# Norm squares, zero masks and a bias of a graph and attention network's heads moved from VectorE to ScalarE and GpSimd

## The chip, the cores and the metric

The kernel runs on one core of a Trainium2 chip. The metric is the device time in microseconds of one execution; lower is better. The engines are named as the profile names them: PE (TensorE, matmuls), DVE (VectorE), ACT (ScalarE), POOL (GpSimd) and SP (SyncE, which here issues most DMAs).

## The reference

A two-layer network on 3327 nodes with 256 features. Layer 0 is a normalised graph convolution and a mixture of eight experts; layer 1 is a graph attention and the attention block that concerns us here. That block, cut to what matters, with 4 heads of width 64, 4 query experts a head, and the length s = 3327:

```
sx = einsum('bsh,ndh->bnsd', x, hl_w) + hl_b          # x is layer-normed first
pad = sx == 0
q, k, v = projections of sx
scores = einsum('bnesd,bntd->bnest', q, k) * d ** 0.5 + causal
qkv = einsum('bnest,bntd->bnesd', softmax(scores), v)
qkv = where(pad[:, :, None], 0.0, qkv)
gs = softmax(einsum('bnsf,nef->bnse', out, gate_w) + gate_b)
mixed = einsum('bnsed,bnse->bnsd', out, gs)
fx = layernorm(mixed + resid, ln_g, ln_b)              # over 64, for each head
pm = fx == 0
hx = relu(where(pm, 0.0, fx @ fc1_w.T + fc1_b))
hx = where(pm, 0.0, hx @ fc2_w.T + fc2_b)
hx = layernorm(hx + fx, fnorm_g, fnorm_b)
fg = softmax(fout @ fgate_w.T)
result = hx * fg, added to x
```

`layernorm` here is (x - mean) / sqrt(mean of squared deviations + 1e-8) over the 64 features of a head.

## The kernel before

The 3327 rows are padded to 26 tiles of 128 rows. The first third of the program does layer 0 and the graph attention of layer 1. The rest, the function `heads`, is what the change touches, and it follows them without overlap but for its constants.

In `heads` a unit is a row tile `t` and a head `h`; tiles go from 0 to 25, and because the attention is causal, tile `t` sees `t + 1` key tiles, which are cut into `t // 4 + 1` chunks of at most 512 keys. One pass of the main loop handles one chunk `k` and issues for it, in this order:

- `drain`: DVE copies the four score banks `pqk` (one for each query expert) from PSUM to the tile `sc` and takes the row maximum in the same instruction. It runs one unit ahead, since the maximum over all chunks of a unit (`anmax`) is needed before the exponentials.
- `attend`: PE multiplies the weights of chunk `k` with the values `vr` into `po`.
- `turn`: DVE transposes the weights of chunk `k + 1` in 32x32 blocks.
- `values` and `weigh`: SP loads `vr` for chunk `k + 2`; ACT computes its exponentials in place, two experts now and two later in the pass.
- if a unit ended in the pass before, `back`: PE turns the unit's output back (`ptO`), and ACT copies it out as `qkv` and `glp`.
- if a unit ends in this pass, `over`: ACT copies `po` to `ot`, and POOL multiplies `ot` by the zero mask `sxd`.
- one step of each open tail and preparation, in passes after which no unit's `back` is due, and in every pass for tiles below 8.
- the second half of `weigh`, and `fill`: PE computes the scores of a later chunk into `pqk`.

A preparation (`prepare`, for the next tile) loads the tile's rows, norms them (`xn`), transposes, projects to `sxt`, and makes keys `kt`, values `v`, queries `qt` and the mask `sxd`. The mask begins as a copy of `sxt` that four DMAs of SP spread over partitions; a DVE comparison with zero then turns it into ones and zeros. A tail (`tail`, for a tile whose four heads are done) is a generator of small steps: gate softmax (`gs`), mix to `fx`, norm `l1`, fully connected layer 1 (`h1`) and 2 (`p2`, `fo`), norm `l2`, final gate (`fg`), store. The last tile has its own `last_tail`, in two halves. As many as five tails are open at once: `back` steps them on while more than four are left, and then opens another.

All engines issue in program order: the class `InOrder` ties each instruction of an engine to the one before it, so an instruction that waits holds up all that follow on its engine. PSUM tiles of `heads` other than `po` rotate through four banks of one tag, which the scores and the small matmuls of tails and preparations share. The function `empty` copies from PSUM either by ACT or by DVE, whichever has the smaller running sum in `load`; the sums are the author's estimates in microseconds, added where instructions are issued:

```
if load["act"] + 0.14 + 0.00086 * n <= load["dve"] + 0.1 + 0.00112 * n:
```

The two norms of a tail (`norm4`) use DVE's statistics instructions, two for each of four heads, and then POOL for the power -0.5, the subtraction, and the three multiplications and additions. The zero masks of the fully connected layers are DVE instructions that compare with zero and multiply at once.

Of the kernel before, what the change touches and what calls it, by code (L numbers as in the profile page):

```python
# [12 lines left out]
F32 = mybir.dt.float32  # L13
# [4 lines left out]
AF = mybir.ActivationFunctionType  # L18
ALU = mybir.AluOpType
AX = mybir.AxisListType  # L20
PSUM = bass.MemoryType.PSUM

P = 128
# [3 lines left out]
D = 256  # L27
# [74 lines left out]
class Net:  # L102
# [766 lines left out]
    def heads(self, xs, vs, out):  # L869
        tc, a = self.tc, self.a  # L870
        nc = InOrder(tc)
        Q = 32
        with ExitStack() as ctx:
            one = ctx.enter_context(tc.tile_pool(name="at", bufs=1))
# [3 lines left out]
            tl = ctx.enter_context(tc.tile_pool(name="att", bufs=2))  # L878
            sm = ctx.enter_context(tc.tile_pool(name="atsm", bufs=4))
# [10 lines left out]
            load = dict(act=0.0, dve=0.0)  # L890

            def empty(dst, src, n, scale=None):
                if load["act"] + 0.14 + 0.00086 * n <= load["dve"] + 0.1 + 0.00112 * n:
                    load["act"] += 0.14 + 0.00086 * n
                    if scale is None:
                        nc.scalar.copy(dst, src)
                    else:
                        nc.scalar.mul(dst, src, scale)
                else:
                    load["dve"] += 0.1 + 0.00112 * n  # L900
                    if scale is None:
                        nc.vector.tensor_copy(dst, src)
                    else:
                        nc.vector.tensor_scalar(dst, src, scale, None, ALU.mult)

            def turned(src, dst):

                pt = ps.tile([P, 2, P], F32, tag="b", name="pt")
                for k in range(2):
                    nc.tensor.transpose(pt[:, k, :], src[:, ts(k, P)], self.ident)  # L910
                empty(dst, pt, D)

            def prepare(t, res):
# [7 lines left out]
                nc.vector.bn_stats(st, x)  # L924
                nc.vector.bn_aggr(mv, st)
                nc.vector.tensor_scalar(rs, mv[:, 1:2], 1e-5, None, ALU.add)
                nc.gpsimd.tensor_tensor(rs, rs, self.nhalf[:, :1], ALU.pow)
                load["dve"] += 0.7
                yield
                xn = self.work.tile([P, D], F32, tag="xn", name="xn2", bufs=1)  # L930
                nc.vector.tensor_scalar(xn, x, mv[:, 0:1], rs, ALU.subtract, ALU.mult)
                load["dve"] += 0.35
                yield
                xt = self.work.tile([P, 2, P], F32, tag="xt", name="xt2", bufs=1)
                turned(xn, xt)
# [8 lines left out]
                for c in range(2):  # L944
                    nc.scalar.activation(
                        sxt[:, c, :], pp[:, c, :], AF.Identity, bias=hlb[:, c : c + 1]
                    )
                load["act"] += 0.6
                yield

                sxd = self.work.tile([P, 4, P], F32, tag="sxd", name="sxd", bufs=3)
                for k in range(2):
                    for s in range(2):
                        nc.sync.dma_start(
                            out=sxd[ds(64 * k, 64), s::2, :], in_=sxt[ds(64 * s, 64), :, :]
                        )
                pp = ps.tile([P, 4, 64], F32, tag="b", name="pv")
                for c in range(2):
# [32 lines left out]
                for s in range(2):  # L991
                    empty(qt[:, s::2, :, :], pp[s], BLK, 8.0)
                yield
                nc.vector.tensor_scalar(sxd, sxd, 0.0, None, ALU.not_equal)
                load["dve"] += 0.4
                sx = tl.tile([P, D], F32, tag="sx", name="sx", bufs=5)
                turned(sxt.rearrange("p c q -> p (c q)"), sx.rearrange("p (c q) -> p c q", c=2))
                res.update(sx=sx, sxd=sxd, qt=qt)
# [80 lines left out]
            def turn(u, g):  # L1079
# [4 lines left out]
                nc.vector.transpose(w, w)  # L1084
                load["dve"] += 0.1 + 0.00417 * n


            po = ps_o.tile([P, 4, BLK], F32, tag="po", name="po")
            po = po[:, :, :P].rearrange("p q (e i) -> p q e i", e=4)
# [54 lines left out]
            def rows(v):  # L1144

                return v.unsqueeze(1).to_broadcast([P, 4, 64])

            def softmax4(g, n, tag):

                g3 = g.rearrange("p (n e) -> p n e", e=4)  # L1150
                m = sm.tile([P, n], F32, tag=tag + "m", name=tag + "m")
                s = sm.tile([P, 4 * n], F32, tag=tag + "s", name=tag + "s")
                s3 = s.rearrange("p (n e) -> p n e", e=4)
                nc.vector.tensor_reduce(m, g3, AX.X, ALU.max)
                nc.vector.tensor_tensor(s3, g3, m.unsqueeze(2).to_broadcast([P, n, 4]), ALU.subtract)
                yield
                nc.scalar.activation(s, s, AF.Exp)
                yield
                nc.vector.tensor_reduce(m, s3, AX.X, ALU.add)
                nc.vector.reciprocal(m, m)  # L1160
                nc.vector.tensor_tensor(s3, s3, m.unsqueeze(2).to_broadcast([P, n, 4]), ALU.mult)
                load["dve"] += 0.6
                load["act"] += 0.25
                return s

            def norm4(v, g, b, tag):

                mv = sm.tile([P, 4, 2], F32, tag=tag + "mv", name=tag + "mv")
                for h in range(4):
                    st = sm.tile([P, 6], F32, tag=tag + "st", name=tag + "st")  # L1170
                    nc.vector.bn_stats(st, v[:, ts(h, 64)])
                    nc.vector.bn_aggr(mv[:, h, :], st)
                rs = sm.tile([P, 4], F32, tag=tag + "rs", name=tag + "rs")
                nc.vector.tensor_scalar(
                    rs, mv.rearrange("p h s -> p s h")[:, 1, :], 1e-8, None, ALU.add
                )
                load["dve"] += 1.1
                nc.gpsimd.tensor_tensor(rs, rs, self.nhalf[:, :4], ALU.pow)
                v3 = v.rearrange("p (h d) -> p h d", h=4)
                nc.gpsimd.tensor_tensor(v3, v3, mv[:, :, 0:1].to_broadcast([P, 4, 64]), ALU.subtract)  # L1180
                nc.gpsimd.tensor_tensor(v3, v3, rs.unsqueeze(2).to_broadcast([P, 4, 64]), ALU.mult)
                nc.gpsimd.tensor_tensor(v3, v3, rows(g), ALU.mult)
                nc.gpsimd.tensor_tensor(v3, v3, rows(b), ALU.add)

            def tail(t, sx, qkv, glp, den):
# [13 lines left out]
                nc.vector.tensor_tensor(gl, gl, gb, ALU.add)  # L1199
                load["dve"] += 0.9  # L1200
                gs = yield from softmax4(gl, 4, "gs")
                nc.vector.tensor_tensor(gs, gs, rd, ALU.mult)
                mx = qkv.rearrange("p h e d -> p (h e) d")
                nc.gpsimd.tensor_tensor(
                    mx, mx, gs.unsqueeze(2).to_broadcast([P, 16, 64]), ALU.mult
# [7 lines left out]
                nc.gpsimd.tensor_tensor(fx, fx, sx, ALU.add)  # L1213
                yield
                yield
                norm4(fx, lng, lnb, "l1")
                yield
                yield
                fxt = tl.tile([P, 2, P], F32, tag="fxt", name="fxt", bufs=2)
                turned(fx, fxt)  # L1220
                yield
                h1 = tl.tile([P, 2, P], F32, tag="h1", name="h1")
                ph = ps.tile([P, 2, P], F32, tag="b", name="ph1")
                for c in range(2):
                    nc.tensor.matmul(ph[:, c, :], fc1, fxt[:, c, :], start=True, stop=True)
                nc.scalar.activation(h1, ph, AF.Relu, bias=fb1)
                load["act"] += 0.4
                yield
                nc.vector.scalar_tensor_tensor(h1, fxt, 0.0, h1, ALU.not_equal, ALU.mult)
                load["dve"] += 0.4  # L1230
                yield
                p2 = ps.tile([P, D], F32, tag="b", name="ph2")
                for c in range(2):
                    nc.tensor.matmul(p2[:, ts(c, P)], h1[:, c, :], fc2, start=True, stop=True)
                fo = tl.tile([P, D], F32, tag="fo", name="fo", bufs=3)
                nc.vector.tensor_tensor(
                    fo.rearrange("p (h d) -> p h d", h=4),
                    p2.rearrange("p (h d) -> p h d", h=4), rows(fb2), ALU.add,
                )
                nc.vector.scalar_tensor_tensor(fo, fx, 0.0, fo, ALU.not_equal, ALU.mult)  # L1240
                load["dve"] += 0.8
                nc.gpsimd.tensor_tensor(fo, fo, fx, ALU.add)
                yield
                yield
                norm4(fo, fng, fnb, "l2")
                yield
                yield
                fot = tl.tile([P, 2, P], F32, tag="fxt", name="fot", bufs=2)
                turned(fo, fot)
                x = tl.tile([P, D], F32, tag="xend", name="xend", bufs=2)  # L1250
                nc.sync.dma_start(out=x, in_=xs[ts(t, P), :])
                yield
                pg = ps.tile([P, 4], F32, tag="b", name="pfg")
# [8 lines left out]
            def last_tail(t, c, sx, r):  # L1262
# [4 lines left out]
                if c == 0:  # L1267
                    r["fx"] = tl.tile([P, D], F32, tag="fx", name="fx", bufs=3)
                    r["fo"] = tl.tile([P, D], F32, tag="fo", name="fo", bufs=3)
                    r["fot"] = tl.tile([P, 2, P], F32, tag="fotl", name="fotl", bufs=1)  # L1270
                    x = r["x"] = tl.tile([P, D], F32, tag="xend", name="xend", bufs=2)
                    nc.sync.dma_start(out=x, in_=xs[ts(t, P), :])
                fx, fo, fot = r["fx"][:, half], r["fo"][:, half], r["fot"][:, c, :]

# [39 lines left out]
                    AX.X, ALU.add,  # L1314
                )
                nc.vector.tensor_tensor(gl, gl, gb[:, ds(8 * c, 8)], ALU.add)
                gs = yield from softmax4(gl, 2, "lgs")
                nc.vector.tensor_tensor(gs, gs, rd, ALU.mult)
                yield
                mx = qkv.rearrange("p h e d -> p (h e) d")  # L1320
# [11 lines left out]
                yield  # L1332
                ph = ps.tile([P, P], F32, tag="b", name="ph1")
                nc.tensor.matmul(ph, fc1, fxt, start=True, stop=True)
                h1 = tl.tile([P, P], F32, tag="h1", name="h1")
                nc.scalar.activation(h1, ph, AF.Relu, bias=fb1)
                yield
                nc.vector.scalar_tensor_tensor(h1, fxt, 0.0, h1, ALU.not_equal, ALU.mult)
# [15 lines left out]
                pg = ps.tile([P, 4], F32, tag="b", name="pfg")  # L1354
                for k in range(2):
                    nc.tensor.matmul(pg, fot[:, k, :], fgw[:, k, :], start=(k == 0), stop=(k == 1))
                fg = yield from softmax4(pg, 1, "fg")
                f3 = fo.rearrange("p (h d) -> p h d", h=4)
                nc.vector.tensor_tensor(f3, f3, fg.unsqueeze(2).to_broadcast([P, 4, 64]), ALU.mult)
                nc.vector.tensor_tensor(fo, fo, x, ALU.add)  # L1360
# [629 lines left out]
```

## Time and profile before

| | us |
|---|---|
| median of 3 runs (3046.64 to 3051.62) | 3050.26 |
| the profiled execution, its own time | 3033.66 |
| its span, first to last instruction | 3032.0 |
| busy in the span: PE / DVE | 2702.8 / 2506.5 |
| busy in the span: ACT / POOL | 1678.2 / 886.5 |

The mean granted TensorE clock of the profiled execution is 0.973. `heads` begins at about 972 us of the span, where the first rows are loaded as `xres`, so it fills about two thirds of it. All instructions of the ordered engines carry line 61 of the program, that of the `InOrder` helper, so groups are told apart by the names of their tiles: `sc<-pqk` is a drain, `sc<-sc` on DVE a transpose and on ACT an exponential, `po<-sc,vr` an attend. A line of a group gives the number of instructions, their busy time, the mean duration in ns, and the idle time of the engine just before them with what ended it. A line of waits gives the total in us, how many there were, and the longest.

### The profile page before, as it was taken

To read this page: it belongs to the slowest core of one execution; us is meant where nothing else is said; L and a number is where in the kernel's file an instruction comes from. 1 tells how busy PE (TensorE), PEld (TensorE's weight loads), DVE (VectorE), ACT (ScalarE), POOL (GpSimd) and SP (SyncE) were. 2 spreads that over 40 slices of the span, in tenths; PEclk is the share of its full clock that TensorE was granted. 3 is DMA by queue.
4 is the path that set the end of the run, shared out by engine and by line. 5 is a ranking of instruction groups with operands and counts; after the bars stand their busy time and mean duration, and the time that the engine had idled before them with its cause. 6 is when DMAs were issued, how large, how long until landed. Compare 5 with 4: busy or idle time off the path is not lost.

```text
span 3032.0 us, 126726 instructions
## 1 busy us (share of the span) xinstructions
PE 2702.8 (89%) x54254; PEld 2004.2 (66%) x54254; DVE 2506.5 (83%) x6203; ACT 1678.2 (55%) x4570; POOL 886.5 (29%) x1178
## 2 busy tenths in 40 slices
PE   7999988788899789998999998899989999999885
PEld 6878877667677666666666666666656666666554
DVE  5103643789997689999999999999999999999996
ACT  6410144555554556565666665666656666566664
POOL 6441644711322254432332221222121111111121
PEclk9999999889999889999999999999999999999998
DMA  9994578567773223333333343333333433433332
GB/s 376 356 314 134 190 240 261 199 212 253 247 266 99 67 74 110 95 95 104 111 99 106 104 120 105 99 111 105 111 107 104 116 107 114 116 111 106 113 106 74
DMA packets 258194, 449.81 MB, mean 148 GB/s; under 512 B 58816, under 2 KB 156608, under 8 KB 257504
## 3 DMA queue, kind: packets, MB, share of 16 engines
q1 hardware_dynamic: 245536, 417.50, 44.6%
q0 software_dynamic: 6576, 18.02, 1.6%
q8 instruction: 428, 7.01, 1.0%
q10 hardware_dynamic: 5520, 6.18, 0.6%
q14 instruction: 134, 1.10, 0.1%
HBM read 393.37 MB, written 25.88 MB: 138 GB/s over the span
## 4 chain that ended last, share of the span: by engine, by line
DVE 48%; PE 19%; issue 2%; ACT 1%; DMA 0%; POOL 0%; SPq 0%; DVEq 0%; POOLq 0%; ACTq 0%
DVE sc L61 40%; PE po L61 7%; PE pqk L61 6%; PE acc L61 2%; PE ptO L61 1%; DVE fo L61 1%; DVE l2mv L61 1%; DVE l1mv L61 1%; ACT sc L61 0%; PE pq L61 0%; DVE anmax L61 0%; DVE gl L61 0%; DVE l2st L61 0%; PE psxt L61 0%; DVE l1st L61 0%
## 5 line engine op out<-in xcount | busy, mean ns | idle before, releaser
L61 ACT ACTIVATE sc<-sc,anmax 128x512 f32<-128x512 f32 (+3 forms) x1568 | 1041.1, 670 | 124.1 <-DVE anmax L61 123.9
L61 DVE TENSOR_SCALAR_CACHE_REDUCE sc<-pqk 128x512 f32<-128x512 f32 (+3 forms) x1568 | 897.9, 626 | 52.8 <-PE pqk L61 50.9
L61 PEld LDWEIGHTS po<-sc,vr 32*64 32x64 f32 x43728 | 666.0, 131 | 337.7 <-DVE sc L61 195.5
L61 PE MATMUL po<-sc,vr 32*64 32x128 f32 x43728 | 769.2, 276 | 117.2 <-DVE sc L61 74.2
L61 PE MATMUL pqk<-kt,qt 64*128 64x512 f32 (+3 forms) x3136 | 800.4, 581 | 44.6 <-DVE sc L61 17.1
L61 DVE STREAM_TRANSPOSE sc<-sc 128x2048 f32<-128x2048 f32 (+3 forms) x392 | 816.1, 2082 | 12.9 <-ACT sc L61 12.9
L61 PEld LDWEIGHTS pqk<-kt,qt 64*128 64x128 f32 x3136 | 314.4, 187 | 232.4 <-issue 80.0
L61 PE MATMUL acc<-wh,p 128*128 128x259 f32 x1352 | 310.0, 387 | 34.6 <-DVE p L61 34.5
L61 PEld LDWEIGHTS acc<-wh,p 128*128 128x128 f32 x1352 | 254.2, 191 | 92.7 <-DVE p L61 51.9
L61 PE MATMUL acc<-y,pan 128*128 128x256 f32 x1352 | 301.3, 382 | 11.9 <-DMA pan<-in_adjt_dram 10.2
L61 POOL TENSOR_TENSOR ot<-ot,sxd 128x512 f32<-128x512 f32 x103 | 131.7, 1279 | 611.1 <-ACT ot L61 600.8
L61 ACT ACTIVATION_READ_ACCUMULATOR sc<-sc,anmax 128x1 f32 x1568 | 302.1, 193 | 0.0
L61 PEld LDWEIGHTS acc<-y,pan 128*128 128x128 f32 x1352 | 256.0, 191 | 52.2 <-issue 17.5
L61 ACT ACTIVATE u<-u,d 128x512 f32<-128x512 f32 (+1 forms) x182 | 125.1, 688 | 159.5 <-DVE u L61 159.3
L61 ACT COPY qkv<-ptO 128x256 f32<-128x256 f32 x104 | 38.7, 373 | 222.9 <-PE ptO L61 222.9
L61 DVE SCALAR_TENSOR_TENSOR u<-bc,d 128x512 f32<-128x512 f32 (+1 forms) x182 | 135.8, 747 | 0.1
L61 DVE SCALAR_TENSOR_TENSOR p<-pan,u 128x512 f32<-128x512 f32 (+1 forms) x182 | 126.4, 694 | 10.0 <-PE acc L61 5.7
L61 PE MATMUL ptO<-igw,ot 128*128 128x68 f32 x832 | 116.4, 284 | 15.6 <-DVE sc L61 11.6
L61 DVE DVE_READ_ACCUMULATOR sc<-pqk 128x1 f32 x1568 | 128.6, 82 | 0.0
L61 PEld LDWEIGHTS ptO<-igw,ot 128*128 128x128 f32 x832 | 102.3, 193 | 34.8 <-issue 20.9
L61 ACT ACTIVATE junk<-ar 128x1664 bf16<-128x1664 f32 x52 | 82.7, 1591 | 66.7 <-DMA ar<-in_adj_dram 65.4
L61 PEld LDWEIGHTS <-own 64*128 64x128 bf16 x832 | 53.7, 95 | 94.5 <-issue 82.9
(324 smaller groups left out, 2872.5 us busy)
## 6 DMA issues: line engine op xcount, KB each, us to landing
vr<-vs SPq DMA_DIRECT2D x976, 128.0 KB, 2.6
ar<-in_adj_dram SPq DMA_DIRECT2D x104, 832.0 KB, 7.8
vr<-vs SPq DMA_DIRECT2D x544, 96.0 KB, 2.2
pan<-in_adjt_dram SPq DMA_DIRECT2D x156, 256.0 KB, 4.7
pan<-in_adjt_dram SPq DMA_DIRECT2D x26, 1024.0 KB, 10.7
pan<-in_adjt_dram SPq DMA_DIRECT2D x20, 832.0 KB, 4.7
w1e<-w SPq DMA_DIRECT2D x59, 256.0 KB, 2.5
took<-places SPq DMA_DIRECT2D x59, 129.0 KB, 5.0
```

Source lines behind the costliest of these rows:

```text
L61: made = make(*args, **kw)
```

## The change

The statistics of the two tail norms are replaced by one DVE sum for each norm (negated), four ACT Squares with accumulation (on 64 x - sum, so without a division first), and two scalings on POOL; the norm becomes a generator with two more steps. Every comparison with zero is made by ACT, as Square of Sign: for the mask `sxd` before the DMAs that spread it (a tile `nz` takes the place of `sxt` as their source), and for `fx` and `fxt` in a tile `nzf`, which POOL then multiplies in. POOL also takes the norming of `xn` (two instructions in place of one), the addition of the bias `fb2`, and three small multiplications of the softmaxes; `p2` is emptied by `empty`. The last tile's tail keeps its own way, with the softmax product on DVE. The tiles `h1` and `xend` have one buffer instead of two, and the last tile's `xend` is loaded by the second half of its tail instead of the first. The estimates added to `load` are changed to match.

```diff
+            def nonzero(dst, src):
+                nc.scalar.activation(dst, src, AF.Sign)
+                nc.scalar.activation(dst, dst, AF.Square)
+                load["act"] += 0.75
...
@@ prepare
                 nc.vector.tensor_scalar(rs, mv[:, 1:2], 1e-5, None, ALU.add)
+                load["dve"] += 0.7
+                yield
                 nc.gpsimd.tensor_tensor(rs, rs, self.nhalf[:, :1], ALU.pow)
-                load["dve"] += 0.7
-                yield
                 xn = self.work.tile([P, D], F32, tag="xn", name="xn2", bufs=1)
-                nc.vector.tensor_scalar(xn, x, mv[:, 0:1], rs, ALU.subtract, ALU.mult)
-                load["dve"] += 0.35
+                nc.gpsimd.tensor_tensor(xn, x, mv[:, 0:1].to_broadcast([P, D]), ALU.subtract)
+                nc.gpsimd.tensor_tensor(xn, xn, rs.to_broadcast([P, D]), ALU.mult)
...
+                nz = self.work.tile([P, 2, P], F32, tag="xn", name="nz", bufs=1)
+                nonzero(nz, sxt)
...
-                            out=sxd[ds(64 * k, 64), s::2, :], in_=sxt[ds(64 * s, 64), :, :]
+                            out=sxd[ds(64 * k, 64), s::2, :], in_=nz[ds(64 * s, 64), :, :]
...
-                nc.vector.tensor_scalar(sxd, sxd, 0.0, None, ALU.not_equal)
-                load["dve"] += 0.4
@@ softmax4 (last=False)
-                nc.vector.tensor_tensor(s3, s3, m.unsqueeze(2).to_broadcast([P, n, 4]), ALU.mult)
-                load["dve"] += 0.6
+                (nc.vector if last else nc.gpsimd).tensor_tensor(
+                    s3, s3, m.unsqueeze(2).to_broadcast([P, n, 4]), ALU.mult
+                )
+                load["dve"] += 0.4
@@ norm4
-                mv = sm.tile([P, 4, 2], F32, tag=tag + "mv", name=tag + "mv")
+                v3 = v.rearrange("p (h d) -> p h d", h=4)
+                ns = sm.tile([P, 4], F32, tag=tag + "ns", name=tag + "ns")
+                nc.vector.tensor_reduce(ns, v3, AX.X, ALU.add, negate=True)
+                load["dve"] += 0.35
+                yield
+                rs = sm.tile([P, 4], F32, tag=tag + "rs", name=tag + "rs")
                 for h in range(4):
-                    st = sm.tile([P, 6], F32, tag=tag + "st", name=tag + "st")
-                    nc.vector.bn_stats(st, v[:, ts(h, 64)])
-                    nc.vector.bn_aggr(mv[:, h, :], st)
-                rs = sm.tile([P, 4], F32, tag=tag + "rs", name=tag + "rs")
-                nc.vector.tensor_scalar(
-                    rs, mv.rearrange("p h s -> p s h")[:, 1, :], 1e-8, None, ALU.add
-                )
-                load["dve"] += 1.1
+                    nc.scalar.activation(
+                        sq, v[:, ts(h, 64)], AF.Square, bias=ns[:, h : h + 1], scale=64.0,
+                        accum_out=rs[:, h : h + 1],
+                    )
+                load["act"] += 1.2
+                yield
+                nc.gpsimd.tensor_scalar(ns, ns, 1 / 64, None, ALU.mult)
+                nc.gpsimd.tensor_scalar(rs, rs, 1 / 64**3, 1e-8, ALU.mult, ALU.add)
                 nc.gpsimd.tensor_tensor(rs, rs, self.nhalf[:, :4], ALU.pow)
-                nc.gpsimd.tensor_tensor(v3, v3, mv[:, :, 0:1].to_broadcast([P, 4, 64]), ALU.subtract)
+                nc.gpsimd.tensor_tensor(v3, v3, ns.unsqueeze(2).to_broadcast([P, 4, 64]), ALU.add)
@@ tail
-                nc.vector.tensor_tensor(gs, gs, rd, ALU.mult)
+                nc.gpsimd.tensor_tensor(gs, gs, rd, ALU.mult)
...
-                norm4(fx, lng, lnb, "l1")
+                yield from norm4(fx, lng, lnb, "l1")
...
                 turned(fx, fxt)
-                yield
-                h1 = tl.tile([P, 2, P], F32, tag="h1", name="h1")
+                nz = tl.tile([P, 2, D], F32, tag="nzf", name="nzf", bufs=1)
+                nonzero(nz[:, 0, :], fx)
+                yield
+                nonzero(nz[:, 1, :], fxt.rearrange("p c q -> p (c q)"))
+                h1 = tl.tile([P, 2, P], F32, tag="h1", name="h1", bufs=1)
...
-                nc.vector.scalar_tensor_tensor(h1, fxt, 0.0, h1, ALU.not_equal, ALU.mult)
-                load["dve"] += 0.4
+                nc.gpsimd.tensor_tensor(
+                    h1, h1, nz[:, 1, :].rearrange("p (c q) -> p c q", c=2), ALU.mult
+                )
...
-                nc.vector.tensor_tensor(
-                    fo.rearrange("p (h d) -> p h d", h=4),
-                    p2.rearrange("p (h d) -> p h d", h=4), rows(fb2), ALU.add,
-                )
-                nc.vector.scalar_tensor_tensor(fo, fx, 0.0, fo, ALU.not_equal, ALU.mult)
-                load["dve"] += 0.8
+                empty(fo, p2, D)
+                f3 = fo.rearrange("p (h d) -> p h d", h=4)
+                nc.gpsimd.tensor_tensor(f3, f3, rows(fb2), ALU.add)
+                nc.gpsimd.tensor_tensor(fo, fo, nz[:, 0, :], ALU.mult)
                 nc.gpsimd.tensor_tensor(fo, fo, fx, ALU.add)
...
-                norm4(fo, fng, fnb, "l2")
+                yield from norm4(fo, fng, fnb, "l2")
...
-                x = tl.tile([P, D], F32, tag="xend", name="xend", bufs=2)
+                x = tl.tile([P, D], F32, tag="xend", name="xend", bufs=1)
```

More of the change, by code (lines that the diff above doesn't have):

```diff
@@ L926, in prepare @@
                 nc.vector.tensor_scalar(rs, mv[:, 1:2], 1e-5, None, ALU.add)
-                nc.gpsimd.tensor_tensor(rs, rs, self.nhalf[:, :1], ALU.pow)
                 load["dve"] += 0.7
                 yield
+                nc.gpsimd.tensor_tensor(rs, rs, self.nhalf[:, :1], ALU.pow)
                 xn = self.work.tile([P, D], F32, tag="xn", name="xn2", bufs=1)
-                nc.vector.tensor_scalar(xn, x, mv[:, 0:1], rs, ALU.subtract, ALU.mult)
-                load["dve"] += 0.35
+                nc.gpsimd.tensor_tensor(xn, x, mv[:, 0:1].to_broadcast([P, D]), ALU.subtract)
+                nc.gpsimd.tensor_tensor(xn, xn, rs.to_broadcast([P, D]), ALU.mult)
                 yield
@@ L1085, in turn @@
                 load["dve"] += 0.1 + 0.00417 * n
+            sq = one.tile([P, 64], F32, name="sq")
             po = ps_o.tile([P, 4, BLK], F32, tag="po", name="po")
@@ L1146, in rows, with softmax4 @@
                 return v.unsqueeze(1).to_broadcast([P, 4, 64])
-            def softmax4(g, n, tag):
+            def softmax4(g, n, tag, last=False):
                 g3 = g.rearrange("p (n e) -> p n e", e=4)
@@ L1166, in norm4 @@
             def norm4(v, g, b, tag):
-                mv = sm.tile([P, 4, 2], F32, tag=tag + "mv", name=tag + "mv")
-                for h in range(4):
-                    st = sm.tile([P, 6], F32, tag=tag + "st", name=tag + "st")
-                    nc.vector.bn_stats(st, v[:, ts(h, 64)])
-                    nc.vector.bn_aggr(mv[:, h, :], st)
-                rs = sm.tile([P, 4], F32, tag=tag + "rs", name=tag + "rs")
-                nc.vector.tensor_scalar(
-                    rs, mv.rearrange("p h s -> p s h")[:, 1, :], 1e-8, None, ALU.add
-                )
-                load["dve"] += 1.1
+                v3 = v.rearrange("p (h d) -> p h d", h=4)
[4 more added lines that the diff above has]
+                rs = sm.tile([P, 4], F32, tag=tag + "rs", name=tag + "rs")
+                for h in range(4):
+                    nc.scalar.activation(
[6 more added lines that the diff above has]
+                nc.gpsimd.tensor_scalar(rs, rs, 1 / 64**3, 1e-8, ALU.mult, ALU.add)
                 nc.gpsimd.tensor_tensor(rs, rs, self.nhalf[:, :4], ALU.pow)
-                v3 = v.rearrange("p (h d) -> p h d", h=4)
-                nc.gpsimd.tensor_tensor(v3, v3, mv[:, :, 0:1].to_broadcast([P, 4, 64]), ALU.subtract)
+                nc.gpsimd.tensor_tensor(v3, v3, ns.unsqueeze(2).to_broadcast([P, 4, 64]), ALU.add)
                 nc.gpsimd.tensor_tensor(v3, v3, rs.unsqueeze(2).to_broadcast([P, 4, 64]), ALU.mult)
@@ L1270, in last_tail @@
                     r["fot"] = tl.tile([P, 2, P], F32, tag="fotl", name="fotl", bufs=1)
-                    x = r["x"] = tl.tile([P, D], F32, tag="xend", name="xend", bufs=2)
+                else:
+                    x = r["x"] = tl.tile([P, D], F32, tag="xend", name="xend", bufs=1)
                     nc.sync.dma_start(out=x, in_=xs[ts(t, P), :])
@@ L1316, in last_tail @@
                 nc.vector.tensor_tensor(gl, gl, gb[:, ds(8 * c, 8)], ALU.add)
-                gs = yield from softmax4(gl, 2, "lgs")
+                gs = yield from softmax4(gl, 2, "lgs", True)
                 nc.vector.tensor_tensor(gs, gs, rd, ALU.mult)
@@ L1334, in last_tail @@
                 nc.tensor.matmul(ph, fc1, fxt, start=True, stop=True)
-                h1 = tl.tile([P, P], F32, tag="h1", name="h1")
+                h1 = tl.tile([P, P], F32, tag="h1", name="h1", bufs=1)
                 nc.scalar.activation(h1, ph, AF.Relu, bias=fb1)
@@ L1356, in last_tail @@
                     nc.tensor.matmul(pg, fot[:, k, :], fgw[:, k, :], start=(k == 0), stop=(k == 1))
-                fg = yield from softmax4(pg, 1, "fg")
+                fg = yield from softmax4(pg, 1, "fg", True)
                 f3 = fo.rearrange("p (h d) -> p h d", h=4)
```

## The prediction

> **What bounds the kernel now.** I read the page's busy shares and slices, then busy time by stage, then the groups and waits of the longest stage, and last a timeline of single instructions.
>
> ```profile
> PE 2702.8 (89%) x54254; PEld 2004.2 (66%) x54254; DVE 2506.5 (83%) x6203; ACT 1678.2 (55%) x4570; POOL 886.5 (29%) x1178
> ...
> DVE  5103643789997689999999999999999999999996
> ...
> POOL 6441644711322254432332221222121111111121
> ```
>
> The mean shares name PE. The slices say otherwise for the last two thirds, which are the heads: there DVE is at 9 and POOL at 1 or 2. Busy time of each engine by stretch (columns PE, PEld, DVE, ACT, POOL):
>
> ```profile
> 960.00:1104.00 144.00, 118.46 (x1816) 92.82 (x1814) 94.02 (x305) 71.79 (x237) 45.52 (x47) 0.86 0.25 68
> 1104.00:1292.00 188.00, 171.59 (x3908) 123.77 (x3907) 172.63 (x515) 115.70 (x368) 95.21 (x110) 0.95 0.33 95
> 1292.00:2879.00 1587.00, 1448.55 (x40788) 987.98 (x40790) 1528.96 (x3676) 997.83 (x2975) 344.15 (x383) 0.99 0.37 108
> 2879.00:3032.00 153.00, 111.00 (x3536) 77.22 (x3534) 127.30 (x302) 81.12 (x241) 26.41 (x33) 0.92 0.31 90
> ```
>
> The third row is tiles 8 to 24, 17 of 26: DVE 96%, PE 91%, ACT 63%, POOL 22%. So DVE bounds it, with PE close behind. Rows 1 and 2 (tiles 0 to 7) have PE level with or above DVE; work taken from DVE there frees little. The waits of DVE, and then of PE, in the third stretch:
>
> ```profile
> DVE sc L61 <- PE pqk L61: 37.1, 51, 3.5
> ...
> PE po L61 <- DVE sc L61: 64.3, 88, 1.5
> PE po L61 <- issue: 19.6, 28, 1.4
> ```
>
> PE waits for DVE more than DVE for PE. Of the 1587 us, DVE has 1529 of work, 37 of waits for PE and 21 of gaps of tens of ns. PE has 1449 + 20 of its own issue gaps. One 512-wide chunk takes DVE 4.67 us (four drains of 0.61 start to start, a transpose of 2.23) and PE 4.08 (attend 2.09, fill 1.99), both read from the timeline at 2218 to 2228 us. What a tail or preparation adds to DVE comes after the transpose and delays the next drain. That is seen at the first norm of a tail:
>
> ```profile
> 2212.39 0.18 DVE L61 BATCH_NORM_STATS2 l1st<-fx 128x6 f32<-128x64 f32 x1
> 2212.61 0.18 DVE L61 BATCH_NORM_AGGREGATE l1mv<-l1st 128x2 f32<-128x6 f32 x1
> ...
> 2213.80 0.17 DVE L61 TENSOR_SCALAR l1rs<-l1mv 128x4 f32<-128x4 f32 x1
> 2213.88 0.68 DVE L61 TENSOR_SCALAR_CACHE_REDUCE sc<-pqk 128x512 f32<-128x512 f32 x1
> ```
>
> Nine small instructions push the drain back by 1.49 us.
>
> **What the Trainium skill says.** "GPSIMD Engine Reference", section Specifications: GpSimd shares its SBUF interfaces with VectorE and contends with VectorE instructions in a two-port mode or with two SBUF inputs. The trace agrees: at 1034.17 us the `gss` multiply on DVE took 1.16 us beside a POOL `ot` multiply of 1034.03 to 1035.31; alone it takes 0.17. Drains from PSUM and transposes keep their 0.61 and 2.23 beside POOL work. "ScalarE: Activation LUTs", section What ACT_TABLE_LOAD costs: an activation is 186 ns + 0.833 ns an element, 93 more for each pointer operand, 93 less back to back. By this a 512-wide Exp is 0.71; the trace has 715 ns. The same page, Table sets: simple functions lie in every set. The trace has five table loads of 1283 ns, none in the heads, and the instruction order of the changed kernel has the same five, so I charge Sign and Square no loads.
>
> **The change part by part**, for one tile in the third stretch.
>
> *Taken from DVE.* Durations are from DVE's groups there, less about 0.08 where an instruction starts inside its predecessor, plus 0.04 for its gap. Norm l1: 1.49. Norm l2: 1.65, as its `rs` averages 0.354 instead of 0.188. `xn` 0.45, `sxd` compare 0.41, `fo` add 0.39, `fo` mask 0.52, `h1` mask 0.40, `fgs` 0.22, `gss` multiplies 0.25 and 0.21. Sum 5.99 us.
>
> *Given to DVE.* Two reduces of 128x256 to 4. No such row exists: the 64-element reduce takes 0.27, the 256-wide statistics 0.40. I take 0.37 each, 0.74. Net 5.25; over 17 tiles 89 us. The balancer also moves 14 evacuations from ACT to DVE by the new order, mostly in tiles 0 to 7: 11 at 0.42 and 3 at 0.69, 6.7 us.
>
> *Given to ACT.* Six 256-wide Sign or Square, by that page's price an estimate of 0.31 to 0.40 each (2.0; a 256-wide copy shows 0.37), eight 64-wide Squares with accumulator at about 0.35 start to start (2.8; the 128-wide Exp with its read goes every 0.40), `fo` evacuation 0.3: 5.1 us a tile, 87 in the stretch. ACT goes from 63% to about 72%. Queued behind them are the second pair of Exps of each iteration, and behind those DVE's transpose; DVE waits 0.7 us in all for Exps now, and an iteration's Exps are 2.84 us of 4.67. If that cover fails, the price is the second rival's.
>
> *Given to POOL.* Two for `xn` (0.62 each by `fx<-fx,l1mv`), three 256-wide (0.73 each), seven tiny ones (0.2 to 0.4 by its one-element rows): 5.4 us a tile, 92 in the stretch, 22% to 29%. Hidden there; the POOL results are wanted one or two iterations later. In tiles 4 to 7 POOL goes from 51% to about 63%, and `ot`, for which the next iteration's `ptO` waits, queues behind tail work.
>
> *New waits.* Each norm has two more steps, so a tail takes 21 steps instead of 17; with at most five open no burst of forced steps arises. ACT's Squares wait for DVE's reduce, issued a step earlier: covered by an iteration. The preparation's `xn` now follows POOL's power and whatever POOL has queued: 0.9 us longer in tile 0, where nothing covers it, 0 to 5 us in tiles 1 to 4. SP issues the same transfers; the four for `sxd` wait 0.7 us longer for ACT, and the single `xend` buffer makes a load wait for the preceding tail's last POOL add. Queued behind both on SP are the `vr` loads, issued two iterations ahead, about 9 us of cover. PSUM: `ph2` is emptied by ACT instead of by DVE after its transpose; PE's fills wait 7.4 us for DVE's `fo` now, so a small gain if ACT is prompt. DVE's `sxd` wait for its DMA (14.6 us in tiles 0 to 2) goes, but PE's `pqk` is late next: the drain after the longest of them waited another 1.3 us for PE. I count 1.
>
> *Sum.* DVE's own need in the stretch: 1587 - 37 - 89 = 1461. PE's: 1449 + 20 and some 4 for ACT and POOL, 1473, an upper bound, since modelled ends stretch some attends (2.46 against 2.09 for the same matmuls). Two engines this even wait more for each other: with the old 37 us kept the stretch is 1461 + 37 = 1498 at best; with PE as the bound and the old 2.4% on it, 1508; tiles 6, 7 and 17, where the two engines are level, ran 4 to 6% over the busier one, which would be 1532 to 1561. I take 1515: 72 saved of 89. Tile 24's tail lies beside tile 25 (DVE 83%): 3. Tiles 0 to 7: DVE loses 7 x 5.3 + 1, gets 6.7, but PE and the latency chain set the pace: -25 to +30, taken as +3. Late Exps and banks: -6, from 0 to -20. Together 72. The profiled execution, 3033.66 us by its own time (span 3032.0), would become 2962; it lies 17 us below the median of 3050.26, so the forecast is **2978 us**.
>
> **The rivals.** *PE is the bound already.* Its 91% is nearly all that its in-order matmuls allow, and DVE's time turns into waits for `pqk`. For: no stretch shows PE above 91%, and tiles 4 to 7 had both at 91%. Against: PE's waits for DVE outnumber the reverse. At 94% PE the stretch is 1541, 46 saved; with 15 lost in the early tiles and on ACT, 31 in all: 3019.
> *Slower: ACT makes the Exps late.* ACT runs in order and waits for PE's `pt`, `ph`, `ptO` in mid-iteration (up to 9 us); the Squares and Signs then stand ahead of the Exps that the next transpose wants. For: ACT would be at about 73% in tiles 4 to 7. Against: 0.7 us of such waits today and a whole iteration of lead. The gain is 78 us, 3.1 a tile, so it decides from 3.1 us of late transposes a tile; at five iterations a tile late by 1 us it is 125 lost, 3050 + 47 = 3097.
> *More than counted*: waits stay at 37 and the contended DVE operations (`l2rs` up to 1.27) free the early tiles: 89 + 3 + 18, 2940.
> *No effect in sum*: early-tile losses of 40 with PE as bound; about 3048.
>
> **How the numbers follow.** Forecast case 0.60 (2955 to 3000), PE bound 0.23 (2995 to 3043), late Exps 0.10, more gain 0.05, none 0.02. The range 2948 to 3043 leaves out late Exps, half of the fifth case and part of the fourth. A measurement tells about 0.2%, 6 us, from no change. Faster 0.86, same 0.03, slower 0.11.
>
> **What would show it.** Right: tiles 8 to 24 in about 1515 us; DVE busy there near 1440, PE's share 94 to 96%; DVE's waits for `pqk` 50 to 70 us; waits of DVE for Exps under 10; two `ns` reduces at 0.3 to 0.4 us; no table load in the heads. Wrong: DVE waiting for ACT `sc` by tens of us (second rival), PE under 92% with long `pqk` waits (first), or tiles 0 to 7 longer than 340 us, against 332 now.

## The result: 41 us faster; in the two profiles, 58 gained late and 36 lost early

The changed kernel takes 3007.36 us (median of 4 runs, 3003.33 to 3012.03), the kernel before in the same comparison 3048.45. The ratio is 0.987, 95% interval 0.984 to 0.990. The two profiled executions are 26.5 us apart by their spans (3032.0 and 3005.5), since the one of before was faster than its median; the accounts below are of these two. In which stretch the other 15 us of the 41 lie, no profile shows.

The page of the changed kernel, to lay beside the lines shown of before:

```profile
PE 2690.0 (90%) x54254; PEld 1992.6 (66%) x54254; DVE 2400.0 (80%) x5617; ACT 1817.4 (60%) x5131; POOL 1003.0 (33%) x1480
...
DVE  5102643689998556888899999999999999999996
...
POOL 5441644612232245544333332232222121122121
```

DVE lost 106 us of work, ACT gained 139, POOL 117. The DVE slices dip to 5 5 6 a third of the way along, where before they had 6 8 9, and POOL has 4 5 5 4 at about the same place, where it had 5 4 4 3. That is where the tiles are short. By stretch, the early tiles and then tiles 8 to 24 (span, then PE, PEld, DVE, ACT, POOL, with the granted PE clock third from the end); the early tiles are counted here from the first statistics of the heads to the start of the last `ot` copy of tile 7:

```profile
975.60:1328.70 353.10, 292.50 (x5654) 213.75 (x5656) 232.72 (x648) 214.42 (x728) 163.69 (x223) 0.85 0.27 76
```

```profile
1328.70:2857.50 1528.80, 1424.86 (x40798) 973.37 (x40796) 1448.54 (x3257) 1100.25 (x3381) 430.94 (x602) 1.00 0.39 112
```

The same early stretch before the change:

```profile
974.60:1291.70 317.10, 277.25 (x5662) 205.95 (x5662) 256.11 (x793) 181.74 (x593) 137.37 (x150) 0.91 0.30 85
```

Tiles 0 to 7 became 36 us longer (317.1 to 353.1) although DVE has 23 us less to do in them. Tiles 8 to 24 became 58 us shorter (1587.2 to 1528.8), tile 25 another 4.7. The same number of PE instructions took 15 us more of PE in the early tiles, at a granted clock of 0.85 instead of 0.91. With about 0.6 us at the two ends the sum is the 26.5.

What PE waited for in the early tiles of the changed kernel (total us, times, longest):

```profile
PE pt L61 <- POOL xn L61: 21.6, 5, 5.8
PE ptO L61 <- POOL ot L61: 13.3, 4, 6.5
```

Before, `ptO` waited most for DVE, and `xn` came from DVE; both waits were shorter:

```profile
PE ptO L61 <- DVE sc L61: 7.0, 6, 2.7
...
PE pt L61 <- DVE xn L61: 3.3, 1, 3.3
```

The longest of the `ot` waits, in the timeline:

```profile
1117.34 0.60 ACT L61 COPY ot<-po 128x512 f32<-128x512 f32 x1
...
1119.56 0.73 POOL L61 TENSOR_TENSOR fx<-fx,lnb 128x256 f32<-128x256 f32 x1
...
1120.85 1.90 POOL L61 TENSOR_TENSOR qkv<-qkv,gss 128x1024 f32<-128x1024 f32 x1
1122.83 1.26 POOL L61 TENSOR_TENSOR qkv<-qkv 128x512 f32<-128x512 f32 x1
...
1124.96 0.72 POOL L61 TENSOR_TENSOR fx<-fx,sx 128x256 f32<-128x256 f32 x1
1125.64 1.26 POOL L61 TENSOR_TENSOR ot<-ot,sxd 128x512 f32<-128x512 f32 x1
...
1126.96 1.98 PE L61 MATMUL ptO<-igw,ot 128*128 128x68 f32 x8 [6.52 <-POOL ot L61]
```

ACT has `ot` ready at 1117.9 us, and POOL reaches it at 1125.6. POOL has no gap of more than 0.1 us from 1116.4 to 1131.0, and `ot` stands at its place in the queue, behind the norm of one older tail (its last step is `fx<-fx,lnb`) and the mix of the next (`qkv<-qkv,gss` to `fx<-fx,sx`). PE, in order, waits 6.5 us for it; ACT is idle for 9.6 us until it can copy `ptO`. The waits of DVE in tiles 8 to 24:

```profile
DVE sc L61 <- PE pqk L61: 60.2, 84, 3.0
DVE sc L61 <- ACT sc L61: 11.2, 17, 1.8
```

They were 37.1 and 0.7 us before.

### The profile page after: what moved, and what is told of

Its sections match the earlier page's. It is cut to its first block, busy times and chain, and to the rows that moved or that the text cites. A ratio compares the mean times of both kernels' runs of the same rounds, so it can differ in the third digit from the quotient of the medians.

```text
span 3005.5 us, 127048 instructions
## 1 busy us (share of the span) xinstructions
PE 2690.0 (90%) x54254; PEld 1992.6 (66%) x54254; DVE 2400.0 (80%) x5617; ACT 1817.4 (60%) x5131; POOL 1003.0 (33%) x1480
## 5 line engine op out<-in xcount | busy, mean ns | idle before, releaser
L61 PEld LDWEIGHTS pqk<-kt,qt 64*128 64x128 f32 x3136 | 307.7, 189 | 203.2 <-issue 81.1
```

Source lines behind the costliest of these rows:

```text
L61: made = make(*args, **kw)
```

## The experiments

Every kernel was compared with the kernel before on its own chip, so changed kernels are compared by their ratios to it; the changed kernel's is 0.987. The totals that were expected beforehand count from its 3007 us. Stage times are from one profile each. How far one profile can be trusted: five profiles whose tiles 8 to 24 have the changed kernel's code or differ from it there in little gave 1526.7 to 1530.5 us for them, and a sixth (`early_old`) 1538.1. Three profiles with the changed kernel's early tiles gave 348.8 to 353.1 us for those, and three with the early tiles of the kernel before 314.3 to 317.1.

**The early tiles as before.** Preparations and tails of tiles 0 to 7 are those of the kernel before.

```diff
-                    tails.append(tail(u["t"], u["sx"], r["qkv"], r["glp"], r["den"]))
+                    tails.append((tail_old if u["t"] < OLD else tail)(u["t"], ...))
...
-                        preps.append(prepare(t + 1, ready.setdefault(t + 1, {})))
+                        preps.append((prepare_old if t + 1 < OLD else prepare)(t + 1, ...))
```

> The changed kernel, with preparations and tails of tiles 0 to 7 as before the change. Theory (the change loses its time in tiles 0 to 7, where POOL, now loaded at up to 65%, holds back PE, and gains it in tiles 8 to 25): tiles 0 to 7 come back from 369 to about 332 us, tiles 8 to 24 stay near 1529, so some 37 us less than the changed kernel, about 2970. Rival (the tail work of the early tiles is only postponed, and the loss reappears after tile 8): 3000 or more.

Measured: 2979.83 us, ratio 0.979 (0.977 to 0.981). Early tiles 315.1 us, tiles 8 to 24 1538.1:

```profile
977.10:1292.20 315.10, 275.02 (x5659) 205.32 (x5660) 256.00 (x791) 182.41 (x595) 137.76 (x151) 0.91 0.30 85
1292.20:2830.30 1538.10, 1426.21 (x40792) 972.11 (x40794) 1456.22 (x3290) 1092.59 (x3344) 420.54 (x578) 1.00 0.38 111
```

The loss is made in the early tiles by their own tails and preparations, and it is not merely postponed. By the ratios some 25 us came back of the 37 that the theory gave, since tiles 8 to 24 took 9 us more. These go with 8 us more work on DVE there (1456.2 against 1448.5); tails of before that are still open when tile 8 begins would bring such work.

**ot of the early tiles on DVE.** Nothing of the change is undone; POOL's queue is relieved of other work.

```diff
-                (nc.vector if u is units[-1] else nc.gpsimd).tensor_tensor(
+                (nc.vector if u is units[-1] or u["t"] < 8 else nc.gpsimd).tensor_tensor(
                     u["ot"], u["ot"],
```

> The changed kernel, with the ot multiply of tiles 0 to 7 on DVE instead of POOL: takes 32 x 1.27 = 41 us off POOL's queue and 0.7 us each onto DVE, which is at 57 to 80% there. Theory (POOL queue): the 13 us of PE's waits for ot and part of those for xn go; tiles 0 to 7 are 10 to 30 us shorter, tiles 8 to 24 unchanged: 2980 to 2997. Rival (PE's cold clock and DVE's evacuations, not POOL): no gain, or slower by the 22 us of DVE work.

Measured: 2979.56 us, ratio 0.980 (0.978 to 0.981). By the ratios that is some 23 us less than the changed kernel, within the 10 to 27 of the theory. The stretch, and PE's remaining wait for POOL in it:

```profile
977.50:1298.10 320.60, 277.85 (x5658) 205.28 (x5658) 248.54 (x679) 213.72 (x727) 131.74 (x198) 0.93 0.30 84
```

```profile
PE pt L61 <- POOL xn L61: 10.8, 3, 4.9
```

The early tiles fell from 353.1 to 320.6 us with 16 us more work on DVE. No wait of `ptO` for POOL is among PE's longest any more, those for `xn`, which POOL still makes, fell from 21.6 to 10.8 us, the clock is at 0.93 and PE's busy time back at 278. So with `ot` taken from POOL nearly all is repaired. It is not a test of the queue alone: the product itself is shorter on DVE (a median of 0.69 us against 1.27), 32 times, and the same edit to the kernel before was not run.

**xn back on DVE**, for all tiles, with POOL's power a step earlier, as before the change.

```diff
...
-                nc.gpsimd.tensor_tensor(xn, x, mv[:, 0:1].to_broadcast([P, D]), ALU.subtract)
-                nc.gpsimd.tensor_tensor(xn, xn, rs.to_broadcast([P, D]), ALU.mult)
+                nc.vector.tensor_scalar(xn, x, mv[:, 0:1], rs, ALU.subtract, ALU.mult)
```

> The changed kernel, with xn normed by DVE in one instruction as before. Theory (POOL queue holds PE): PE's 22 us of waits for xn in tiles 0 to 7 go, tiles 0 to 7 are 10 to 22 us shorter; tiles 8 to 24 get 17 x 0.45 = 8 us of DVE work back: 3007 - 10 = 2997 in sum, between 2990 and 3003. Rival (the early loss is the balancer's: evacuations on DVE wait for PE): tiles 0 to 7 within 5 us of 369, the whole 3010 or more.

Measured: 3003.05 us, ratio 0.988 (0.986 to 0.989), which is not distinguishable from the changed kernel; the 10 us that the theory took off the whole did not show. Its profile has the early tiles at 340.3 us, 13 less, as the theory had them, with the 13.3 us of waits for `ot` unchanged, and tiles 8 to 24 at 1528.9: there the 7 us of DVE work put back cost nothing visible. In that profile the heads begin 6 us later (first statistics at 981.8 us, not 975.6), after work that the edit does not touch.

**All evacuations on ACT.**

```diff
-                if load["act"] + 0.14 + 0.00086 * n <= load["dve"] + 0.1 + 0.00112 * n:
+                if True:
```

> The changed kernel, with every evacuation of the balancer on ACT: 23 fewer copies on DVE, most in tiles 0 to 7. Theory (POOL queue): little, within 8 us of 3007 either way, since DVE's waits for pk, pv and pt (42 us in tiles 0 to 7) only take the place of waits of ACT. Rival (the evacuations moved to DVE hold back its drains): tiles 0 to 7 shorter by 15 us or more.

Measured: 3011.39 us, ratio 0.990 (0.988 to 0.991), not clearly apart from the changed kernel; early tiles 352.8 us. The rival falls: DVE's waits for `pk`, `pv` and `pt`, 42 us in the changed kernel's early tiles, are a symptom.

**Both reliefs together.** `ot` of tiles 0 to 7 and `xn` of tiles 0 to 8 on DVE, the rest as changed.

```diff
+                if t <= 8:
+                    nc.vector.tensor_scalar(xn, x, mv[:, 0:1], rs, ALU.subtract, ALU.mult)
+                else:
...
+                (nc.vector if u is units[-1] or u["t"] < 8 else nc.gpsimd).tensor_tensor(
```

> The changed kernel with both reliefs of POOL in the early tiles: ot of tiles 0 to 7 and xn of tiles 0 to 8 on DVE. Theory (PE's 11 us of waits for xn that remained with ot on DVE go too): tiles 0 to 7 from 321 (first statistics to last ot copy) to 305 to 315, tiles 8 to 24 as in the changed kernel, 2965 to 2976 in sum. Rival (DVE, at 80 to 90% in tiles 4 to 7, takes over as the bound): 2980 or more.

Measured: 2977.95 us, ratio 0.978 (0.974 to 0.981), 70 us less than before and the lowest median, but not separable from the two kernels above.

```profile
980.90:1299.00 318.10, 277.81 (x5658) 205.45 (x5658) 251.51 (x688) 213.47 (x727) 120.60 (x180) 0.93 0.31 85
```

The early tiles took 318.1 us, 3 to 13 more than the theory gave, and the total lies between its 2976 and the rival's 2980. PE's waits for POOL's `xn` are gone, but nearly nothing came of it. PE has the same 278 us to do, 87% of the stretch, and no engine has more there. What sets its length now was not tested.

**Work added, to price DVE and PE in tiles 8 to 25.** To the kernel before and to the changed one alike, either a DVE reduce after each chunk's drains or four matmuls of zeros in each fill was added (344 reduces and as many fills, not the 376 that the expectations give).

```diff
...
+                if u["t"] >= 8:
+                    nc.vector.tensor_reduce(
+                        spare, u["mx"][:, :, : g + 1], AX.X, ALU.max, negate=True
+                    )
```

```diff
...
+                    for k in range(2 if t >= 8 else 0):
+                        r = ds(64 * k, 64)
+                        nc.tensor.matmul(
+                            pq[2 * i + k][:, n - P : n], own[1][r, :], zero[r, :],
+                            start=False, stop=not last,
+                        )
```

DVE, to the kernel before:

> The kernel before, with one more DVE reduce of the running maxima (0.17 us, result unused) after the drains of each chunk of tiles 8 to 25: 376 of them, about 0.10 us each net of overlap, 38 to 60 us of DVE work. Theory (before the change DVE is the bound there): 0.8 to 1 of it appears, tiles 8 to 25 longer by 35 to 60 us. Rival (PE is already the bound): less than half.

DVE, to the changed kernel:

> The changed kernel, with the same extra DVE reduce. Theory (after the change DVE and PE bound tiles 8 to 25 together): 0.5 to 0.85 of what the same reduces cost in the kernel before. Rival (DVE is still the only bound): the same as there.

PE, to the kernel before:

> The kernel before, with four more matmuls of zeros (bf16, 128 columns, added to the scores) in each fill of tiles 8 to 25: by the mask matmuls' 0.27 us for eight, about 0.14 us a fill, 376 fills, 50 us of PE work. Theory (DVE is the bound, PE has 5% slack): less than half appears, 0 to 25 us. Rival (PE is the bound): 35 us or more.

PE, to the changed kernel:

> The changed kernel, with the same zero matmuls. Theory (bound together): clearly more than in the kernel before, 20 to 40 us. Rival (DVE still the only bound): the same as in the kernel before.

| added | busy, tiles 8 to 24 | tiles 8 to 24 longer by | ratio to before (interval) |
|---|---|---|---|
| DVE, kernel before | 41.6 | 44.0 | 1.0135 (1.0109 to 1.0161) |
| DVE, changed kernel | 43.3 | 33.4 | 1.0008 (0.9997 to 1.0019) |
| PE, kernel before | 37.5 | 8.0 | 1.0027 (1.0015 to 1.0038) |
| PE, changed kernel | 39.1 | 9.5 | 0.9906 (0.9877 to 0.9934) |

To the DVE rows about 10 us of gaps are to be added (0.03 us an instruction), so that 0.86 of the added DVE time appeared before and 0.63 after by the profiles, where the first is measured from the one profile of before, which lies below its median. By the ratios the addition cost the changed kernel 1.4% (1.0008 over 0.9872), as much as before. PE's share is a fifth to a quarter in both. My theory that the two engines bound the changed kernel together is not borne out: PE's price should have risen clearly and did not. DVE still bounds it. Whether its price fell, these runs leave open.

**The parts of the change, one at a time.** The three patches are hunks of the change itself: norms; masks with bias and `fo`; `xn` with the small products. All three keep the single buffers of `h1` and `xend`, which were not tried alone; `early_old` has them too, with early tiles as before. For the norms alone, for instance, the rest of the changed kernel is put back:

```diff
-                nonzero(nz, sxt)
...
-                nc.gpsimd.tensor_tensor(xn, xn, rs.to_broadcast([P, D]), ALU.mult)
...
-                (nc.vector if last else nc.gpsimd).tensor_tensor(
```

> Of the change, only the tail norms (sum on DVE, Squares on ACT, scalings on POOL); masks, bias, xn and the small products on DVE as before. DVE's net in tiles 8 to 24 is 17 x 2.4 = 41 us. Theory (DVE's time is worth 0.65 to 0.85 there, and the early loss is POOL's queue, to which the norms add only about 0.8 us a tile): tiles 8 to 24 in 1552 to 1562 us, tiles 0 to 7 within 10 us of the kernel before. Rival (the two extra steps of each norm lengthen the early tails and make the early loss): tiles 0 to 7 longer by 20 us or more.

> Of the change, only the masks (Square of Sign on ACT, products on POOL) and the bias and evacuation of fo; norms, xn and the small products as before. DVE's net in tiles 8 to 24 is 17 x 1.7 = 29 us, POOL gets 2.2 us a tile. Theory: tiles 8 to 24 in 1562 to 1569 us, tiles 0 to 7 longer by 0 to 12 us. Rival (the Signs and Squares that stand ahead of Exps on ACT are what limits the late gain): tiles 8 to 24 at 1575 or more, with DVE's waits for Exps above 10 us.

> Of the change, only xn and the three small softmax products on POOL. DVE's net in tiles 8 to 24 is 17 x 1.1 = 19 us. Theory: tiles 8 to 24 in 1571 to 1575 us; tiles 0 to 7 longer by 8 to 20 us, since the preparation's xn queues on POOL behind tail work and PE's transpose waits for it. Rival (POOL's queue hurts only with all parts together): tiles 0 to 7 within 5 us of the kernel before.

| part | ratio (interval) | tiles 0 to 7 | tiles 8 to 24 | DVE net, as reckoned |
|---|---|---|---|---|
| norms | 0.988 (0.984 to 0.992) | +11.6 | -31.5 | -41 |
| masks, bias | 0.996 (0.995 to 0.997) | +3.1 | -10.2 | -29 |
| xn, small products | 1.000 (0.999 to 1.002) | +8.9 | -1.5 | -19 |
| sum of the three | | +23.6 | -43.2 | -89 |
| the whole change | 0.987 (0.984 to 0.990) | +36 | -58.4 | -89 |

The norms alone bring about the whole net gain; the masks a little; `xn` and the small products nothing.

The norms' early loss lies between theory and rival. `ptO` waits 11.1 us for POOL's `ot`, so the queue is in it, but not by the amount of its work. These are the early tiles with the norms alone and with the masks alone; the POOL figure is the fifth after the span:

```profile
980.70:1309.40 328.70, 283.21 (x5656) 208.34 (x5658) 248.38 (x690) 201.15 (x692) 138.00 (x169) 0.90 0.30 81
```

```profile
980.00:1300.10 320.10, 282.98 (x5659) 208.73 (x5660) 250.16 (x773) 197.55 (x636) 148.62 (x168) 0.90 0.30 84
```

With the norms POOL has 138.0 us to do, against 137.4 before; with the masks it has 148.6, and `ptO` waits only 1.6 us for `ot`. What the norms changed is the order in the queue. First POOL with the norms alone at the last unit of tile 3, then at the same unit before the change:

```profile
1119.47 0.79 POOL L61 TENSOR_TENSOR fx<-fx,lnb 128x256 f32<-128x256 f32 x1
1120.23 1.90 POOL L61 TENSOR_TENSOR qkv<-qkv,gss 128x1024 f32<-128x1024 f32 x1
...
1125.03 1.26 POOL L61 TENSOR_TENSOR ot<-ot,sxd 128x512 f32<-128x512 f32 x1
```

```profile
1099.68 1.30 POOL L61 TENSOR_TENSOR ot<-ot,sxd 128x512 f32<-128x512 f32 x1 [12.80 <-ACT ot L61]
1100.95 1.90 POOL L61 TENSOR_TENSOR qkv<-qkv,gss 128x1024 f32<-128x1024 f32 x1
...
1105.76 1.28 POOL L61 TENSOR_TENSOR ot<-ot,sxd 128x512 f32<-128x512 f32 x1
```

The program says why. A tail's norm used to come two steps after its mix; with the two steps more its POOL part comes four steps after. Tiles 0 to 3 have four passes each, with a step in every one, so the norm of one tail now falls into the pass of the next tail's mix and stands ahead of it. A norm whose steps are spaced otherwise was not run.

For the masks tiles 8 to 24 took 1577.0 us, where the rival had them (1575 or more) and not the theory, but the rival's sign is absent: DVE's waits for Exps were 3.8 us. For `xn` alone the theory's early loss came, though tiles 8 to 24, at 1585.7, missed its 1571 to 1575. PE waited 20.2 us for `xn` on POOL in the early tiles:

```profile
PE pt L61 <- POOL xn L61: 20.2, 6, 4.9
```

The parts lose less early, and gain less late, than all together. Why work removed in pieces of 0.2 to 0.5 us paid less than the norms' block of 1.5 us in front of a drain was not settled. Profiles of like code differ by 3 to 4 us in a stretch, and for tiles 8 to 24 there is only one of the kernel before; by the ratios the norms' gain stands clear, and a small one of the masks.

## Why the prediction was right, and where it was off

The forecast was 2978 us; 3007 came, within the range and in the direction forecast, with 41 us of the 72. That is in part luck: 3007 lies outside the forecast case's own 2955 to 3000, and inside the 2995 to 3043 of the first rival, whose reason did not hold. By the two profiles tiles 8 to 24 gave 58 of the 72 us reckoned for them, and the early tiles, which stood in the sum with a gain of 3, lost 36.

*What bounds it, and DVE's own need*: right. Without its waits for PE and ACT, DVE needs 1528.8 - 60.2 - 11.2 = 1457 us in tiles 8 to 24, and 1461 was reckoned. The reduces that had no row came at 377 and 389 ns against 0.37 us, the table loads stayed five, POOL's share there was 28% (29 reckoned).

*The stretch at 1515*: right in mechanism, off in size by 14 us. The term that was too small is the waits: 54 us were reckoned, 37 of before and 17 more; 71 came, 60 for PE, within the 50 to 70 given as a sign, and 11 for Exps, just over the 10. ACT's cost was too small as well, 6.0 us a tile (102 in 17) instead of 5.1:

```profile
L61 ACT ACTIVATE sq<-fx,l1ns 128x64 f32<-128x64 f32 x68 | 23.7, 348 | 2.4 <-DVE l1ns L61 0.7
L61 ACT ACTIVATE nzf<-fx 128x256 f32<-128x256 f32 x18 | 7.6, 422 | 0.0
L61 ACT ACTIVATE nz<-nz 128x256 f32<-128x256 f32 x17 | 7.1, 416 | 0.5
```

A Sign or Square of 256 elements takes 0.42 us; I had taken an estimate of 0.31 to 0.40 from the Trainium skill ("ScalarE: Activation LUTs", What ACT_TABLE_LOAD costs). Its 0.833 ns an element and 186 ns give 0.40 for one alone, which is near; the overlap of 93 ns that I took off is absent where the Square needs the Sign's result, 0.45 start to start at 1129.67 and 1130.12 us. The Squares with accumulation follow each other by 0.47 us, not 0.35.

*Tiles 0 to 7 at +3, from -25 to +30*: this step failed, and the sign that the text gave for it came: counted as there from 960 us, these tiles took 369 us, over 340. They lost 36 us, outside the term's own bounds. The text named each piece: `xn` behind POOL's queue, 0.9 us in tile 0 and up to 5 in tiles 1 to 4, and `ot` behind tail work, for which `ptO` waits. But it priced only the first and gave the second none, and it let DVE's saving stand against them where DVE, as it said itself, is not the bound. PE's waits came to 21.6 us for `xn` and 13.3 for `ot`. It sought the second in tiles 4 to 7, by POOL's share; the 6.5 us came at the end of tile 3, by the order of the queue. It had counted the two steps more in each norm, but asked only for bursts of forced steps, and not what the norm would then stand beside. `early_old` shows that the early tails and preparations make the loss, `norms_only` against `masks_only` that the wait for `ot` comes with the norms and not with POOL's load.

*The late Exps*, the rival on the slow side: its sign appeared at 11 us in sum, far from the 3.1 us a tile from which it would decide.

*PE as the bound*, the first rival, gave 3019 for 15 us lost early and 31 net. Its early loss did occur, larger, but its reason did not hold: PE's added work cost a quarter of itself. That its number is the nearer one says nothing for it.

*More than counted*, where waits stay at 37 us, did not happen. PE's share in tiles 8 to 24 was 93%, below the 94 to 96 forecast, since the stretch was longer.

## What to carry to other kernels

Price a move to an idle engine stage by stage, and in the stage where that engine is busiest look at what stands behind the moved work in its queue. The amount of work alone does not tell: with the norms alone POOL had 0.6 us more to do in the early tiles, and yet held the matmuls back by up to 5.4 us at a time, since a step more or less decides which instructions stand one behind the other. Where the same loop runs over short and long passes, the assignment of work to engines may differ between them; here `ot` on DVE for the first eight tiles alone was worth some 23 us by the ratios. And take removed work at less than its duration on an engine that has another close behind it: 58 of 89 us here, by the two profiles.

## What the runs showed of the hardware

In the early tiles the same matmuls took 292 us of PE at a granted clock of 0.85 while POOL held them back, and 278 at 0.93 with `ot` on DVE; before the change it was 277 at 0.91. So PE's busy time grew with its waits here; the clock and the busy time did not move in step, and how one makes the other is not shown. On POOL a product of 4 to 16 elements took 0.20 to 0.23 us, a 128x4 power 1.04, a product of 256 elements 0.61 to 0.73 and one of 1024 1.90: the small ones cost little there, and the others make the queue.
